# A four-stage chain on one core: the values of the first batch ahead of its scores, its silu behind the first sum, and the branch numbers chosen one batch later

## The chip, the cores and the metric

The kernel runs on one core of a Trainium2 chip. The metric is the device time of one execution in microseconds (us), as the median of several runs. The engines are named as the profile names them: PE (TensorE, matrix products; PEld is its weight load), DVE (VectorE), ACT (ScalarE), POOL (GpSimd) and SP (SyncE, which issues most of the DMAs). Each engine works through its own queue in order.

## The reference

The reference passes `x`, 16 batches of 256 tokens by 256 features in float32, through four layers. Cut to what matters:

```python
# layer 0: adapter with one of 16 experts per batch, then layer norm
hidden = gelu(x @ down_W.T + down_b)
hidden = hidden @ expert_W[idx].T + expert_b[idx] + domain_emb[idx]
x = layernorm(hidden @ up_W.T + up_b + x) * ln_gamma + ln_beta
# layer 1: conditioned transformer block, 16 heads of 16
emb = silu(sin_emb(timestep)) @ W_ada + b_ada         # sin and cos of 128 angles
scale, shift = split(emb, 2)
x = ln(x) * (1 + scale) + shift
q, k, v = x @ Wq + bq, x @ Wk + bk, x @ Wv + bv
scores = q k^T / 4 + attention_bias; masked with -inf  # the bias is 16 x 256 x 256 per batch
x = x + softmax(scores) v @ Wo + bo
h = ln(x) * g2 + beta2
x = x + gelu2(h @ W1 + b1) @ W2 + b2                   # 1024 hidden
# layer 2: one of three branches per batch (two or three products), then layer norm
x = layernorm(x + branch[condition](x)) * gamma + beta
# layer 3: finite differences along both axes, one time step
out = maximum(f + dt * df(f), 0)
```

## The kernel before

Each batch is held as two halves of 128 tokens by 256 features. The work is written as generators, each of which runs over the batches: `adapt` (layer 0, two batches at a time: matmuls into p_h, p_e and p_u, and the sum `x <- p_u, x`), `prepare` (both layer norms), `project` (transposition c_t, then queries c_q, keys c_k and values c_v), `weigh` (scores c_s for four heads at a time, the bias added and the maximum taken on DVE, the exponential on ACT), `attend` (transposition of the weights into c_pt, its copy c_pts, and the product c_c with the values c_va), `divide` (the softmax's denominator and the product with Wo), `enter` and `feed` (the feed-forward part), `end` (layer 2) and `step` (layer 3). A "quarter" of a batch is the four heads that one turn of `weigh` takes.

The order of the instructions on every engine is fixed while the program is built. `Flow.run` is a small planner: it keeps a clock for each engine with the costs that the generators state (`flow.pe(1.75)`), and picks the next generator among those whose condition holds and whose data and PSUM bank are due. Among these the smallest priority goes first. Each generator is added with a start priority and a number by which its priority grows with the PE time that it has used:

```python
    flow.add(adapt(), -3.31, 1.2)
    flow.add(enter(), -0.18, 0.44)
    flow.add(step(), 4.65, 7.0)
```

So a changed start number, or a changed cost stated to the planner, moves instructions of every generator from there on. The planner also chooses by its clocks whether DVE or ACT does certain operations: the normalization (`normalized`, L433 on DVE or L438 on ACT), the copy out of a transposition (`taken_up`, L472 or L474) and the bias of the feed-forward part (L940 or L938).

The places that the change touches:

- `timestep()` (L358 to L364) computes sine, cosine and tanh on ACT and then, on DVE, the two instructions that make the silu of the embedding (L362, L363). `adapt` calls it for the first pair, ahead of p_u, so the two DVE instructions stand ahead of the first sum (L582). The silu is what the matmuls of `condition` (L500, into ps_a) wait for.
- `choose()` turns the 16 branch numbers into row indices and selected biases, with 13 small DVE instructions (in the profile: L284 to L289 with c_f and c_row, L975 to L985). `prepare` calls it in its turn for batch 1, ahead of that batch's statistics. Its results are read by `load_branch(0)`, which `weigh` calls after the last quarter of batch 0, and by `end`.
- `weigh` begins with batch b once ("prepare", b) is done; `project` sets this after the keys, and ("values", b) after the values. So the scores of the first quarter can stand ahead of the values' product:

```python
            if m % 4 == 0:
                yield lambda: ("prepare", b) in done
```

Batch 0's scores start with matmuls that add the mask (L735, with ident_b). For later batches the mask is added to the bias tiles (`side`) in memory, by DMAs that POOL issues (L517). POOL also adds up_b to each x (`biased`, L529) once its load has landed, and takes the reciprocal square roots of the layer norms (L421 to L425, with tiles rs and nb).

The matmuls named `idle` (L222) multiply zeros while PE has nothing else to do.

Of the kernel before, what the change touches and what calls it, by code (L numbers as in the profile page):

```python
# [170 lines left out]
def chain_kernel(ctx: ExitStack, tc: tile.TileContext, t: dict, out: bass.AP):  # L171
# [3 lines left out]
    flow = Flow(BANKS)  # L175
# [15 lines left out]
    def chunked(w):  # L191
        return w.rearrange("(k p) n -> p k n", p=P)
# [3 lines left out]
    def misc(name, shape):  # L196
        numbers[name] = n = flow.take()
        return pp.tile(shape, F32, name=name, tag=f"m{n}")

    def free(name, at):  # L200

        flow.free_at[numbers.pop(name)] = at
        return at
# [29 lines left out]
    def columns(name):  # L233
        return cols[:, COLUMN[name][0] : COLUMN[name][1]]
# [6 lines left out]
    def load_turned(p):  # L241

        arrives["t", p] = flow.clock["PE"] + 9.0 if p else 0.0
        xts[p] = xp.tile([P, 2, NC, S], F32, name=f"xt{p}", tag="xt", bufs=1)
        for i in range(2):
            nc.sync.dma_start(out=xts[p][:, i], in_=chunked(t["x_t"][2 * p + i]))
# [111 lines left out]
    def timestep():  # L358
        for i, red in enumerate((sine, cosine)):
            nc.scalar.activation(emb[:, i, :], red, AF.Sin)  # L360
        nc.scalar.activation(th, emb, AF.Tanh, scale=0.5)
        nc.vector.tensor_scalar(emb, emb, 0.5, None, ALU.mult)  # L362
        nc.vector.scalar_tensor_tensor(silu, th, 1.0, emb, ALU.add, ALU.mult)  # L363
        flow.dve(0.25, flow.act(3.4))  # L364


    rows_a = load("rows_a", rows(t["rows_a"]), [P, 5 * D])
# [12 lines left out]
    def spread_mask(b):  # L380
        negs[b] = wp.tile([P, NC, S], BF16, name=f"neg{b}", tag="neg", bufs=2)
        nc.gpsimd.tensor_scalar(negs[b], m8s.pop(b), MASKED, None, ALU.mult)
        flow.pool(1.6)
# [96 lines left out]
    done = set()  # L480
    ready, ys, stats2, lns, hts, stats3 = {}, {}, {}, {}, {}, {}

    def expert_bias():

        ps_b = misc("ps_b", [2 * A, B // 2])
        for i in range(2):
            half = ps_b[i * A : (i + 1) * A, :]
            nc.tensor.matmul(half, e_rows[:, :A], e_hot[: E + 2, i::2], start=True, stop=False)
            nc.tensor.matmul(half, e_rows[:, A:], e_hot[: E + 2, i::2], start=False, stop=True)
        nc.vector.tensor_copy(e_add, ps_b)  # L490
        return free("ps_b", flow.dve(0.2, flow.pe(0.5)))
# [35 lines left out]
    def biased(b):  # L527
        x = xs[b]
        nc.gpsimd.tensor_tensor(x, x, up_b.unsqueeze(1).to_broadcast([P, NC, D]), ALU.add)  # L529
        flow.pool(1.35, arrives["x", b])  # L530
        done.add(("x", b))

    def adapt():

        for p in range(B // 2):
            yield lambda: p in e_ws and (p == 0 or ("normal", 1) in done)
            yield arrives.get(("t", p), 0.0)
            parts = [slice(i * A, (i + 1) * A) for i in range(2)]
            w, xt = e_ws.pop(p), xts.pop(p)
            ps_h = misc(f"p_h{p}", [2 * A, S])  # L540
            for k in range(NC):
                for i in range(2):
                    nc.tensor.matmul(
                        ps_h[parts[i]], w_down[:, k, :], xt[:, i, k, :], start=k == 0, stop=k == NC - 1
                    )
            h1 = xp.tile([2 * A, S], F32, name=f"a_h1{p}", tag="a_h1", bufs=1)
            nc.scalar.activation(h1, ps_h, AF.Gelu, bias=columns("down_b"))
            at = free(f"p_h{p}", flow.act(0.47, flow.pe(1.0), "gelu"))
            if p == 0:
                nc.scalar.dma_start(out=w_qkv, in_=chunked(t["W_qkv"]))  # L550
                expert_bias()
            yield at
            if p == 0:
                biased(0)
                spread_mask(0)
            ps_e = misc(f"p_e{p}", [2 * A, S])
            for i in range(2):
                nc.tensor.matmul(ps_e[parts[i]], w[parts[i]], h1[parts[i]], start=True, stop=True)
            h2 = xp.tile([2 * A, S], F32, name=f"a_h2{p}", tag="a_h2", bufs=1)
            nc.vector.tensor_scalar(h2, ps_e, e_add[:, p : p + 1], None, ALU.add)  # L560
            at = free(f"p_e{p}", flow.dve(0.4, flow.pe(0.5)))
            if p and 2 * p + 2 < B:
                load_turned(p + 1)
                load_expert(p + 1)
            if p:
                yield lambda: ("x", 2 * p + 1) in done
            yield at, 2
            if p == 0:
                timestep()
                idle(256)  # L570
            ps_u = [misc(f"p_u{2 * p + i}", [P, NC, D]) for i in range(2)]
            for c in range(NC):
                for i in range(2):
                    nc.tensor.matmul(
                        ps_u[i][:, c, :], h2[parts[i], c * P : (c + 1) * P], up[parts[i]], start=True, stop=True
                    )
            at = flow.pe(1.0)
            for b in (2 * p, 2 * p + 1):
                if b == 1:
                    yield lambda: ("normal", 0) in done  # L580
                x = xs[b]
                nc.vector.tensor_tensor(x, ps_u[b % 2], x, ALU.add)  # L582
                adapted[b] = free(f"p_u{b}", flow.dve(0.7, at))
                done.add(("adapt", b))
                yield 0.0, 0

    def prepare():
        for b in range(B):
            yield lambda: ("adapt", b) in done
            x, at = xs.pop(b), adapted.pop(b)  # L590
            yield at, 0
            flow.spent += 0.75
            if b + 2 < B:
                load_x(b + 2)
                if b == 0:
                    load_turned(1)
                    load_expert(1)
            if b == 1:
                choose()
            stat, at = take_stats(f"0_{b}", x, at)  # L600
            if b == 0:
                condition()
                idle(512, 512, 512, 512)
            yield at, 0
            tmp = xp.tile([P, NC, D], F32, name=f"b_tmp{b}", tag="b_tmp", bufs=1)
            at = normalized_affine(x, x, stat, ln0_g, ln0_b, tmp, b == 0)
            yield at, 0
            stat, at = take_stats(f"1_{b}", x, at)
            if b == 0:
                conditioned()  # L610
                masked.update((m, 0.0) for m in range(4))
            yield at, 0
            if b > 1:
                yield lambda: ("turned", b - 2) in done
            ln = xp.tile([P, NC, D], F32, name=f"c_ln{b}", tag="c_ln", bufs=2)
            lns[b] = ln, normalized(ln, x, stat, b == 0)
            flow.spent += 1.5
            for n in (1, 2) if b == 0 else (b + 2,) if b + 2 < B else ():
                biased(n)
            done.add(("normal", b))  # L620
# [98 lines left out]
    def weigh():  # L719

        at = 0.0
        for m, (b, half, par) in enumerate(QUADS):
            if m % 4 == 0:
                yield lambda: ("prepare", b) in done
            _, qz, k_t, _, sums = ready[b]
            ps = []
            for i in range(4):
# [159 lines left out]
    def enter():  # L887
        for b in range(B):
            yield lambda: ("finish", b) in done
            stat, at = stats2.pop(b)  # L890
            yield at, 0
            y = ys[b]
            ln = hp.tile([P, NC, D], F32, name=f"d_ln{b}", tag="d_ln", bufs=1)
            yield normalized(ln, y, stat)
            if b > 1:
                yield lambda: ("widen", b - 2) in done
            ps_t = misc(f"d_t{b}", [P, NC, S])
            at = transposed(ps_t, ln)
            h_t = hp.tile([P, NC, S], F32, name=f"d_ht{b}", tag="d_ht", bufs=2)
            for k in range(NC):  # L900
                nc.scalar.activation(
                    h_t[:, k, :], ps_t[:, k, :], AF.Identity, bias=ln2_b[:, k : k + 1], scale=ln2_g[:, k : k + 1]
                )
            for c in range(NC):
                nc.gpsimd.tensor_tensor(y[:, c, :], y[:, c, :], b2, ALU.add)
                flow.pool(0.7)
            hts[b] = h_t, free(f"d_t{b}", flow.act(0.9, at))
            done.add(("enter", b))
# [263 lines left out]
            free(f"e_d{b}", at)  # L1172
            done.add(("step", b))

    flow.add(adapt(), -3.31, 1.2)
    flow.add(prepare(), -2.34, 2.25)
    flow.add(project(), -0.45, 5.7)
    flow.add(weigh(), 0, 21.2)
    flow.add(attend(), 0.9, 11.3)
    flow.add(enter(), -0.18, 0.44)  # L1180
    flow.add(feed(), 2.55, 13.9)
    flow.add(end(), 3.08, 3.95)
    flow.add(step(), 4.65, 7.0)
    flow.run()

def _arrays(inputs):
# [79 lines left out]
```

## Time and profile before

| | |
|---|---|
| time, median of 3 runs | 912.29 us (911.93 to 915.16) |
| the profiled execution: its time | 912.22 us |
| the profiled execution: its span, first to last instruction | 910.4 us |
| mean granted PE clock | 0.990 |
| PE busy | 869.3 us (95%) |
| DVE busy | 636.2 us (70%) |
| ACT busy | 544.1 us (60%) |
| POOL busy | 377.4 us (41%) |
| moved by DMA | 163.25 MB, mean 179 GB/s |

A line of the timeline gives the start and the length in us, the engine, the line of the kernel, the operation, the tile written and the tiles read (`out<-in`) with shapes, and how many instructions were merged (x4). In brackets stands the idle time of the engine ahead of it and what ended that idle time. A line of the table by stage gives the stretch, its length, the busy time of each engine with the number of instructions, and at the end the granted PE clock, the mean busy share of the DMA engines and GB/s. Buffer numbers are left out of tile names.

### The profile page before, as it was taken

What the parts mean: (1) busy time and instruction counts of PE and PEld (TensorE: products, weight loads), DVE (VectorE), ACT (ScalarE), POOL (GpSimd) and SP (SyncE); (2) the same over time, 40 slices, a digit from 0 to 9 for tenths busy, and PEclk for the clock granted to TensorE, in tenths of its full rate; (3) what the DMA queues carried; (4) which work ended last, traced back from release to release, by engine and by line L of the source; (5) the groups of instructions that cost most, each with busy time, mean ns of one, the idle gap of its engine ahead of it and who ended that gap; (6) DMA issues with size and microseconds to landing.
All of it is one profiled execution on the core that took longest, in us unless ns stands there. A gap on an engine that the chain in (4) does not pass through costs nothing. (4 is left out here: it accounts for less than half of the span.)

```text
span 910.4 us, 18249 instructions
## 1 busy us (share of the span) xinstructions
PE 869.3 (95%) x6184; PEld 668.7 (73%) x6184; DVE 636.2 (70%) x2087; ACT 544.1 (60%) x1537; POOL 377.4 (41%) x514
## 2 busy tenths in 40 slices
PE   7889998999999999999999999999999999999996
PEld 3557676777878777676877777787778778776875
DVE  5677867778777867757758686866768676767443
ACT  2576857576664767557765665847557474756230
POOL 3353455445416353351627245542446332422231
PEclk9999999999999999999999999999999999999998
DMA  8599977777888668778478777765857776670000
GB/s 274 166 267 316 285 166 191 183 200 191 203 204 201 179 166 221 217 185 209 125 191 222 179 193 175 190 166 161 195 152 181 180 203 173 176 190 31 13 30 23
DMA packets 130973, 163.25 MB, mean 179 GB/s; under 512 B 12714, under 2 KB 94780, under 8 KB 130876
## 3 DMA queue, kind: packets, MB, share of 16 engines
q0 software_dynamic: 31680, 62.92, 34.0%
q1 hardware_dynamic: 97920, 96.92, 33.5%
q10 hardware_dynamic: 1275, 2.19, 0.7%
q8 instruction: 52, 0.85, 0.4%
q14 instruction: 46, 0.37, 0.1%
HBM read 94.89 MB, written 4.19 MB: 109 GB/s over the span
## 5 line engine op out<-in xcount | busy, mean ns | idle before, releaser
L769 ACT ACTIVATE c_pr<-c_sc,c_mx 128x256 f32<-128x256 f32 x512 | 255.2, 500 | 207.5 <-DVE c_mx L758 203.9
L758 DVE CUSTOM_DVE_ANT_0 c_sc<-c_s,side 128x256 f32<-128x256 f32 x512 | 193.8, 417 | 35.7 <-PE c_s L740 20.2
L472 DVE COPY c_pts<-c_pt 128x512 f32<-128x512 f32 x206 | 137.0, 683 | 21.8 <-PE c_pt L464 21.2
L464 PE MATMUL c_pt<-ident,c_pr 128*128 128x128 f32 x1024 | 144.7, 278 | 7.4 <-ACT c_pr L769 3.6
L464 PEld LDWEIGHTS c_pt<-ident,c_pr 128*128 128x128 f32 x1024 | 114.3, 141 | 43.3 <-issue 14.5
L421 POOL TENSOR_SCALAR rs<-mv 128x2 f32<-128x2 f32 x64 | 14.2, 222 | 279.7 <-DVE mv L418 278.9
L924 PE MATMUL d_f<-d_ht,w 128*128 128x256 f32 x512 | 122.9, 383 | 4.0 <-DVE c_mx L758 2.2
L954 PE MATMUL d_o<-w,d_z 128*128 128x256 f32 x512 | 116.3, 381 | 0.1
L517 POOL DMA_DIRECT2D side<-neg x60 | 82.2, 1379 | 76.6 <-DMA side<-in_side 48.9
L924 PEld LDWEIGHTS d_f<-d_ht,w 128*128 128x128 f32 x512 | 92.7, 190 | 18.7 <-DVE c_mx L758 3.7
L954 PEld LDWEIGHTS d_o<-w,d_z 128*128 128x128 f32 x512 | 94.9, 190 | 14.5 <-issue 1.9
L769 ACT ACTIVATION_READ_ACCUMULATOR c_pr<-c_sc,c_mx 128x1 f32 x512 | 96.2, 188 | 0.0
L740 PE MATMUL c_s<-c_kt,c_qz 32*128 32x256 f32 x1024 | 77.6, 401 | 4.8 <-DVE x L582 1.9
L823 PE MATMUL c_c<-c_pts,c_va 128*32 128x256 f32 x1024 | 74.1, 386 | 2.7 <-DVE c_pts L472 2.5
L740 PEld LDWEIGHTS c_s<-c_kt,c_qz 32*128 32x128 f32 x1024 | 48.9, 184 | 24.5 <-issue 9.7
L962 DVE SCALAR_TENSOR_TENSOR y<-d_o,y 128x256 f32<-128x256 f32 x32 | 13.6, 425 | 63.3 <-PE d_o L954 63.3
L823 PEld LDWEIGHTS c_c<-c_pts,c_va 128*32 128x32 f32 x1024 | 27.9, 109 | 36.9 <-issue 17.9
L943 ACT ACTIVATE d_f<-d_z 128x512 f32<-128x512 f32 x64 | 38.3, 598 | 27.0 <-DVE d_z L940 26.3
L940 DVE TENSOR_SCALAR d_z<-d_f,cols 128x256 f32<-128x256 f32 x94 | 41.0, 477 | 16.2 <-PE d_f L924 16.0
L422 POOL TENSOR_TENSOR rs<-rs,inv_sqrt 128x2 f32<-128x2 f32 x64 | 45.9, 717 | 5.3
L947 DVE SCALAR_TENSOR_TENSOR d_z<-d_f,d_z 128x512 f32<-128x512 f32 x64 | 43.4, 677 | 1.8 <-ACT d_f L943 1.8
L1029 POOL TENSOR_TENSOR y<-y,d_bout 128x256 f32<-128x256 f32 x32 | 23.6, 790 | 47.1 <-PE d_t L464 32.1
(156 smaller groups left out, 1539.7 us busy)
## 6 DMA issues: line engine op xcount, KB each, us to landing
side<-in_side SPq DMA_DIRECT2D x256, 256.0 KB, 5.3
side<-neg POOLq DMA_DIRECT2D x60, 1024.0 KB, 8.1
d_w<-in_W_branch SPq DMA_DIRECT2D x16, 512.0 KB, 4.4
xt<-in_x_t SPq DMA_DIRECT2D x16, 256.0 KB, 6.1
x<-in_x SPq DMA_DIRECT2D x16, 256.0 KB, 5.9
out<-e_o SPq DMA_DIRECT2D x15, 256.0 KB, 3.7
w<-in_W SPq DMA_DIRECT2D x2, 1024.0 KB, 7.5
d_bout<-in_bl_branch SPq DMA_DIRECT2D x16, 128.0 KB, 4.5
```

The source lines that it names most:

```text
L422: nc.gpsimd.tensor_tensor(rs, rs, inv_sqrt, ALU.pow)
L464: nc.tensor.transpose(ps[:, k, c * P : (c + 1) * P], src[:, c, k * P : (k + 1) * P], ident)
L472: nc.vector.tensor_copy(dst, ps)
L517: nc.gpsimd.dma_start(out=sides[m].rearrange("p (h c) k -> p h (c k)", h=HB), in_=negs[m // 4].rearrange("p c k -> p (c k)").unsqueeze(1). ...
L740: nc.tensor.matmul(ps[i][:, c, :], qz[rows32, par, half, c * P : (c + 1) * P], k_t[rows32, half, :], start=b > 0, stop=b > 0 or c == NC - 1,)
L758: nc.vector.tensor_tensor_reduce(out=sc[:, c, :], in0=ps[i][:, c, :], in1=sb[:, i * NC + c, :], scale=-1.0, scalar=3.0e38, op0=ALU.add, op ...
L769: nc.scalar.activation(pr[:, c, :], sc[:, c, :], AF.Exp, bias=mx[:, c : c + 1], scale=-1.0, accum_out=sums[:, c, h : h + 1],)
L823: nc.tensor.matmul(ps_c[32 * i : 32 * i + 32, :], va[:, k, 4 * half + i, 2 * par : 2 * par + 2, :].rearrange("p e d -> p (e d)"), turned[i ...
L924: nc.tensor.matmul(ps_f[:, i, :], w1[:, k, f * P : (f + 1) * P], h_t[:, k, :], start=k == 0, stop=k == NC - 1,)
L940: nc.vector.tensor_scalar(z[:, i, :], ps_f[:, i, :], b1[:, f : f + 1], None, ALU.add)
L947: nc.vector.scalar_tensor_tensor(z, ps_f, 1.0, z, ALU.add, ALU.mult)
L954: nc.tensor.matmul(ps_o, us[f // 2][:, f % 2, c * P : (c + 1) * P], w2[:, f, :], start=f == 0, stop=f == NF - 1,)
```

## The change

The two DVE instructions of the silu are taken out of `timestep()` into a function `silus()`, which `adapt` calls behind the sum of batch 0. `choose()` is called in `prepare`'s turn for batch 2 instead of batch 1. `weigh` begins with batch 0 once its values are done; for the other batches its condition is the same. Three start numbers of the planner are changed. The costs stated to the planner for the silu are split in the same way: ACT's 3.4 stays in `timestep()`, DVE's 0.25 moves, and no longer waits for ACT's clock. The numbers and shapes of the matmuls and of the DMAs stay the same; across DVE and ACT, the planner's choice between the two changes for some instructions.

```diff
@@ -359,9 +359,12 @@
         for i, red in enumerate((sine, cosine)):
             nc.scalar.activation(emb[:, i, :], red, AF.Sin)
         nc.scalar.activation(th, emb, AF.Tanh, scale=0.5)
+        flow.act(3.4)
+
+    def silus():
         nc.vector.tensor_scalar(emb, emb, 0.5, None, ALU.mult)
         nc.vector.scalar_tensor_tensor(silu, th, 1.0, emb, ALU.add, ALU.mult)
-        flow.dve(0.25, flow.act(3.4))
+        flow.dve(0.25)
@@ -580,6 +583,8 @@
                 x = xs[b]
                 nc.vector.tensor_tensor(x, ps_u[b % 2], x, ALU.add)
+                if b == 0:
+                    silus()
                 adapted[b] = free(f"p_u{b}", flow.dve(0.7, at))
                 done.add(("adapt", b))
                 yield 0.0, 0
@@ -595,7 +600,7 @@
                 if b == 0:
                     load_turned(1)
                     load_expert(1)
-            if b == 1:
+            if b == 2:
                 choose()
             stat, at = take_stats(f"0_{b}", x, at)
@@ -721,7 +726,7 @@
         for m, (b, half, par) in enumerate(QUADS):
             if m % 4 == 0:
-                yield lambda: ("prepare", b) in done
+                yield lambda: ("prepare" if b else "values", b) in done
             _, qz, k_t, _, sums = ready[b]
@@ -1172,15 +1177,15 @@
-    flow.add(adapt(), -3.31, 1.2)
+    flow.add(adapt(), -3.24, 1.2)
     flow.add(prepare(), -2.34, 2.25)
     flow.add(project(), -0.45, 5.7)
     flow.add(weigh(), 0, 21.2)
     flow.add(attend(), 0.9, 11.3)
-    flow.add(enter(), -0.18, 0.44)
+    flow.add(enter(), -0.02, 0.44)
     flow.add(feed(), 2.55, 13.9)
     flow.add(end(), 3.08, 3.95)
-    flow.add(step(), 4.65, 7.0)
+    flow.add(step(), 4.83, 7.0)
```

## The prediction

> **What bounds the kernel now.** I read the page's engine row, then a table of TensorE's (PE) busy time by stage, then the timeline of the stage that the change touches.
>
> ```profile
> PE 869.3 (95%) x6184; PEld 668.7 (73%) x6184; DVE 636.2 (70%) x2087; ACT 544.1 (60%) x1537; POOL 377.4 (41%) x514
> ```
>
> ```profile
> 21.00:100.00 79.00, 69.49 (x518) 0.96 0.87 258
> ...
> 850.00:910.40 60.40, 50.69 (x248) 0.94 0.07 24
> ```
>
> ```profile
> 100.00:850.00 750.00, 732.74 (x5363) 572.22 (x5362) 541.77 (x1770) 474.49 (x1356) 318.72 (x420) 1.00 0.71 181
> ```
>
> PE is the bound. After the stretch come its length, PE's busy time and, at the row's end, the granted clock and DMA. PE idles 9.5 us from 21 to 100, 17.3 us in all of 100 to 850, 9.7 us in the last 60. The change leaves the number of matmuls as it is, so it can only move these idle pieces and the slow-clock stretches. Now the opening, with what each gap waited for in brackets:
>
> ```profile
> 13.54 0.18 DVE L362 TENSOR_SCALAR smalls<-smalls 128x32 f32<-128x32 f32 x1 [1.95 <-ACT smalls L361]
> ...
> 13.86 0.68 DVE L582 TENSOR_TENSOR x<-p_u,x 128x512 f32<-128x512 f32 x1
> ...
> 26.35 1.27 POOL L529 TENSOR_TENSOR x<-x,rows_a 128x512 f32<-128x512 f32 x1 [3.80 <-DMA x<-in_x]
> ...
> 28.75 0.73 DVE L433 TENSOR_SCALAR b_tmp<-x,mv,rs 128x256 f32<-128x256 f32 x2 [1.21 <-POOL rs L422]
> ...
> 32.12 0.76 DVE L700 TENSOR_TENSOR c_va<-c_v,rows_a 128x256 f32<-128x256 f32 x2 [1.17 <-PE c_v L691]
> ```
>
> ```profile
> 29.01 1.15 PE L740 MATMUL c_s<-c_kt,c_qz 32*128 32x256 f32 x16 [1.71 <-ACT c_kt L679]
> 30.09 1.99 PE L691 MATMUL c_v<-w_qkv,c_xt 128*128 128x256 f32 x8
> 31.92 0.60 PE L464 MATMUL c_pt<-ident,c_pr 128*128 128x128 f32 x4
> 34.96 0.33 PE L464 MATMUL c_pt<-ident,c_pr 128*128 128x128 f32 x1 [2.44 <-ACT c_pr L769]
> ...
> 63.60 0.33 PE L464 MATMUL c_t<-ident,c_ln 128*128 128x128 f32 x1 [1.20 <-ACT c_ln L438]
> ...
> 66.50 1.57 PE L823 MATMUL c_c<-c_pts,c_va 128*32 128x256 f32 x10 [1.29 <-DVE c_pts L472]
> 67.99 3.12 PE L648 MATMUL c_q<-c_xt,w_qkv 128*128 128x256 f32 x8
> ```
>
> Three waits of the first batch are named: scores for keys (1.71), the second transposition for its softmax (2.44), and on VectorE (DVE) the first sum behind the silu, which stands for 1.95 behind ScalarE's (ACT's) tanh.
>
> **The change, part by part.** (x(n) is batch n's activations, weigh(m,i) head i of quarter batch m.)
>
> *Silu behind the first sum.* The sum's inputs are there at 12.61 (POOL's add, 11.35 + 1.26) and 12.78 (PE's p_u, 11.64 + 1.14), so it runs from about 12.8 instead of 13.86. The silu pair (0.32) then stands at 13.54 as before, since tanh ends at 13.50; the statistics start near 13.95 instead of 14.58: 0.63 won on DVE and POOL. On PE it is worth less. The warm-up matmuls (L222, idle) hold PE from 15.92 to 21.17, and the first transposition c_t began at 21.16; only its wait for the second half goes. I take 0.2 for PE (bounds 0 and 0.63).
>
> *Branch numbers out of batch 1.* `choose()` held DVE from 23.19 to 25.49: 2.30 us ahead of x(1)'s statistics, themselves ahead of c_qz. Without it c_qz starts when c_q is there, about 24.5 instead of 26.57, and the keys' copy c_kt near 26.4 instead of 28.49. But x(1) gains nothing from it: POOL's rs for x(1) is queued behind POOL's add for x(2), and that waits for x(2)'s DMA until 26.35, which no part of the change moves. So b_tmp stays at 28.75 and x(1) is normalized at 32.19 as now.
>
> *Values ahead of the scores.* c_v (2.0 on PE) goes to where PE waited for keys: c_k ends near 26.2, c_v 28.0, the mask matmuls 29.0, the scores run 29.0 to 30.0: their start stays within 0.1 us of the 29.01 of before. So the 1.71 is filled, but c_v no longer covers the softmax after it: PE idles from 30.0 until c_pr is exponentiated at 31.7. DVE then does c_va (29.45), weigh(0,0) at 30.2 (30.18 before), x(1)'s second statistics at 32.25, bound by POOL's 32.19, and weigh(0,1) at 33.35 (33.87 before). The order now has weigh(0,2) directly behind, at 34.05 instead of 35.13, and c_ln of x(1) comes at 35.4 instead of 36.64. On ACT two table loads and a gelu (1.28 + 0.47 + 1.28) stay ahead of the fourth exponential. PE's p_h of the next pair is moved into the softmax wait (from 35.92 to about 32.3).
>
> *The clock.* These rows show PE's busy time right after the stretch's length, and the granted clock as the third number from the end.
>
> ```profile
> 28.00:32.00 4.00, 2.99 (x25) 2.38 (x26) 1.51 (x6) 2.42 (x8) 3.48 (x5) 1.00 0.04 9
> 32.00:36.00 4.00, 1.40 (x11) 0.80 (x11) 3.71 (x15) 1.50 (x5) 1.90 (x6) 1.00 0.00 0
> 36.00:40.00 4.00, 4.00 (x21) 2.82 (x22) 2.71 (x8) 3.94 (x8) 0.87 (x1) 0.57 0.15 50
> ```
>
> In 36 to 40 the clock is 0.57, and there p_h takes 1.78 (1.08 at 54.43) and c_t 1.06 (0.66 at 89.79). [...] The longest gap here is 2.44[...]. After the change PE is busy about 2.0 us of 32 to 36 (rest of a transposition, p_h, another one), against 1.40 before and 2.61 in 64 to 68, which was followed by 0.71 in 68 to 72. I therefore let c_t and the mask of the next quarter run slow again. Worked through to c_k of batch 1 (45.84 before), the lead is 1.2 us by the row; with full clock[...], 2.1. I take 1.2 and keep 2.1 for the range.
>
> *Branch numbers into batch 2.* The same 2.30 us of DVE, no DMA of its own, now stand between weigh(1,3) and x(2)'s statistics, about 47.4 to 49.7. Queued behind are those statistics, the copy c_pts of a transposition and weigh(2,0), near 51.5 instead of 52.26. PE had no idle worth a bracket from 43 to 63, and DVE is busy 12.33 of 15 there, so I charge 0.3 (bounds 0 and 1.2). SP issues the load of x(4) behind four side loads and w2 instead of ahead of them: near 51.5 and not 45.04. It lands in about 6.0, and POOL adds to x(4) only at 61.46; I cost that nothing. Without that cover of some 4 us POOL, and the mask addition queued behind it there, would be late by what is missing.
>
> *The order after that.* The planner's costs and the three start numbers (adapt, enter, step) move nearly every row from there on. In the order after the change the second batch's gather c_c stands ahead of c_t of x(2), not behind it, and c_ln of x(2) is done on DVE, not on ACT behind eight exponentials. So c_c and more transpositions cover the 1.36 us wait for c_ln (1.20 and 0.16). What is at stake from 57 to 76 is that, the 1.29 for c_pts and 1.13 of slow clock in c_q (3.12 against 1.99): 3.8 us. I take 2.6, bounds 0 and 3.8. From 100 to 850 DVE gets 18 more instructions (8 normalizations of 0.365, 5 copies of 0.683, one of 0.69, 4 bias adds of 0.477: 8.9 us) and ACT as many fewer. PE's listed waits there name DVE for 10.1 us and ACT for 4.1, in pieces of at most 1.9, so no row tells a sign: I take 0, bounds -6 and +8. The last 157 matmuls, from batch 14's output product on, stand in the same order in both: 0.
>
> **Sum.** -1.2 + 0.3 - 2.6 = -3.5 us. The profiled execution took 912.22 (span 910.4 and 1.8 around it), 0.07 under the median of 912.29; so 908.7.
>
> **The rivals.** *The middle falls well too.* The new order loses less than the 17.3 us of 100 to 850: with 5 us fewer 903.7. For it: the pieces are accidents of order, and ACT, relieved of 18 instructions, answers sooner. Against: DVE pays for that.
>
> *The lead is handed back.* The masked sides, or w1 and w2, arrive when they did: DMA's share is 1.02 in 57 to 76 and 1.09 in 76 to 100. Then little but 0.7 us remains: 911.5. Against it: no PE gap from 21 to 100 names a DMA.
>
> *DVE late, slower.* `choose()` in front of x(2)'s statistics delays the weighing that all PE work of the second batch needs, by its whole 2.30 less the lead of 1.2, the gains at 57 to 76 do not come, and the 8.9 us of DVE work moved from ACT raise PE's waits on DVE (10.1) by half: 1.1 + 5 = 6.1, 918.3. It decides once PE's waits on DVE in 100 to 850 pass about 14 us. For it: DVE is the releaser in most of them, and 203.9 us of ACT's waiting are for DVE's c_mx. Against: DVE is idle 28% of that stretch.
>
> *Nothing of what it says.* Weigh(0,0) stays at 30.2 and x(1) stays bound by x(2)'s DMA; if the clock dips longer as well, the opening gives nothing. This lies in the second rival's figure.
>
> **How the numbers follow.** 0.5% (4.6 us), about what a measurement of this kernel can tell from no change, puts the bounds at 907.7 and 916.9. The likeliest, 0.46, is 908.7 with its own range 904.5 to 912.5: 0.20 faster, 0.25 same, 0.01 slower. Middle falls well 0.20, all faster. Lead handed back 0.09: 0.08 same, 0.01 slower. DVE late 0.25: 0.23 slower, 0.02 same. Together 0.40, 0.35 and 0.25. The range, 900 to 920, takes in the full clock and the bounds of the middle down to -5 and up to about +8.
>
> **What would show it.** Right: c_v between c_k and the mask matmuls with no gap; scores near 29.0; weigh(0,1) near 33.4; POOL's x(2) still waiting for DMA near 26.35; the third quarter's scores 1 to 2 us under 51.0; PE idle from 21 to 100 near 7 instead of 9.5. Wrong: PE idle in 100 to 850 away from 17.3 by over 5, which would outweigh the opening; or PE waiting for c_mx or c_pts between 47 and 60.

## The result, and the profile after

The changed kernel takes 918.44 us (median of 5 runs, 916.23 to 921.17); the kernel before, beside it, 912.27 (5 runs, 910.42 to 915.16). The ratio is 1.0059 with a 95% interval of 1.0035 to 1.0083: slower, by 6.2 us at the medians. The forecast was 908.7.

The profiled execution of after was the longest of its five, 921.17 (span 919.4). From the page, the engine row first:

```profile
PE 872.3 (95%) x6184; PEld 668.7 (73%) x6184; DVE 648.3 (71%) x2105; ACT 535.5 (58%) x1519; POOL 377.0 (41%) x514
```

The span is 9.0 us longer than before's 910.4. PE's busy time accounts for 3.0 of it (872.3 against 869.3). The matmuls are the same 6184, and this part is slow clock: the stretches at half clock cost PE 11.2 us in this trace and 8.2 in before's. PE's idle time accounts for the other 6.0 (919.4 - 872.3 = 47.1, against 41.1), which is about the difference of the medians. The 18 instructions that left ACT for DVE are there (2105 and 1519). The table by stage, for PE alone (length, busy time, then granted clock, DMA share and GB/s), of before and then of after:

```profile
21.00:42.00 21.00, 16.04 (x105) 0.92 0.47 144
42.00:57.00 15.00, 14.71 (x118) 1.00 0.88 291
57.00:76.00 19.00, 16.26 (x118) 0.91 1.02 265
76.00:100.00 24.00, 22.50 (x184) 1.00 1.09 330
170.00:850.00 680.00, 665.69 (x4887) 1.00 0.70 179
```

```profile
21.00:42.00 21.00, 16.41 (x106) 0.92 0.49 150
42.00:57.00 15.00, 13.62 (x106) 1.00 0.92 294
57.00:76.00 19.00, 16.40 (x141) 1.00 0.88 235
76.00:100.00 24.00, 21.82 (x168) 1.00 1.09 326
170.00:850.00 680.00, 661.91 (x4855) 1.00 0.70 180
```

Length less busy time is PE's idle time. From 21 to 42 it falls by 0.4 us; then it rises by 1.1, falls by 0.1 and rises by 0.7. So the opening, which was to gain, has 1.2 us more idle PE by 100 than before. From 170 to 850 it rises from 14.3 to 18.1. The rest (to 21, from 100 to 170, behind 850) adds 0.8, 0.0 and 0.2; the 0.8 need not come of the change, since e11 below, with before's instructions up to 32, idles 6.5 to 21, against before's 4.6.

The opening in after's timeline, first DVE, then POOL, then PE:

```profile
12.77 0.69 DVE L585 TENSOR_TENSOR x<-p_u,x 128x512 f32<-128x512 f32 x1 [1.56 <-POOL x L532]
...
26.90 1.27 POOL L532 TENSOR_TENSOR x<-x,rows_a 128x512 f32<-128x512 f32 x1 [5.24 <-DMA x<-in_x]
...
29.29 0.73 DVE L436 TENSOR_SCALAR b_tmp<-x,mv,rs 128x256 f32<-128x256 f32 x2 [4.13 <-POOL rs L425]
```

```profile
25.69 1.89 PE L696 MATMUL c_v<-w_qkv,c_xt 128*128 128x256 f32 x8
27.42 1.04 PE L740 MATMUL c_s<-neg,ident_b 128*128 128x256 bf16 x8
28.38 1.15 PE L745 MATMUL c_s<-c_kt,c_qz 32*128 32x256 f32 x16
31.72 0.33 PE L467 MATMUL c_pt<-ident,c_pr 128*128 128x128 f32 x1 [2.19 <-ACT c_pr L774]
...
50.11 1.15 PE L745 MATMUL c_s<-c_kt,c_qz 32*128 32x256 f32 x16
52.28 0.63 PE L467 MATMUL c_pt<-ident,c_pr 128*128 128x128 f32 x4 [1.02 <-DVE c_pts L475]
```

The values stand without a gap ahead of the mask matmuls, and the scores start 0.6 us sooner than before. PE then waits 2.19 for the softmax. At 50.11 the third quarter's scores are 0.9 us ahead of before's 51.0. Behind them is a wait that before did not have: 1.02 for DVE. The cause is on DVE:

```profile
48.09 0.17 DVE L284 CAST c_f<-tok 128x16 f32<-128x16 int32 x1
...
49.97 0.51 DVE L990 SCALAR_TENSOR_TENSOR b_sel<-is_c,cols,b_sel 128x16 f32<-128x16 f32 x2
50.39 0.42 DVE L420 BATCH_NORM_STATS2 st<-x 128x6 f32<-128x256 f32 x1
...
51.47 0.66 DVE L475 COPY c_pts<-c_pt 128x512 f32<-128x512 f32 x1
```

`choose()` holds DVE for 2.30 us, and the copy that PE waits for is queued behind it and the statistics.

### The profile page after: what moved, and what is told of

Read it like the earlier page. It is cut to its first block, busy times and chain, and to the rows that moved or that the text cites. A ratio compares the mean times of both kernels' runs of the same rounds, so it can differ in the third digit from the quotient of the medians.

```text
span 919.4 us, 18249 instructions
## 1 busy us (share of the span) xinstructions
PE 872.3 (95%) x6184; PEld 668.7 (73%) x6184; DVE 648.3 (71%) x2105; ACT 535.5 (58%) x1519; POOL 377.0 (41%) x514
## 3 DMA queue, kind: packets, MB, share of 16 engines
q10 hardware_dynamic: 1275, 2.19, 0.7%
## 5 line engine op out<-in xcount | busy, mean ns | idle before, releaser
L467 PE MATMUL c_pt<-ident,c_pr 128*128 128x128 f32 x1024 | 147.1, 278 | 13.2 <-ACT c_pr L774 5.6
L475 DVE COPY c_pts<-c_pt 128x512 f32<-128x512 f32 x211 | 140.4, 683 | 14.6 <-PE c_pt L467 14.3
```

The lines of the kernel that those rows point to most:

```text
L467: nc.tensor.transpose(ps[:, k, c * P : (c + 1) * P], src[:, c, k * P : (k + 1) * P], ident)
L475: nc.vector.tensor_copy(dst, ps)
```

## The experiments

Kernels of one group share a chip and their runs of before. "In before's order" means that the costs told to the planner stay as in before, so every instruction that is not moved by hand keeps its place on every engine.

**e1_starts**: before, with only the three start numbers of the change.

```diff
-    flow.add(adapt(), -3.31, 1.2)
-    flow.add(enter(), -0.18, 0.44)
-    flow.add(step(), 4.65, 7.0)
+    flow.add(adapt(), -3.24, 1.2)
+    flow.add(enter(), -0.02, 0.44)
+    flow.add(step(), 4.83, 7.0)
```

> The kernel before with only the three new start numbers (adapt, enter, step); the first batch's instructions stand as before. Theory A (the order of everything behind the first batch costs the time, and the start numbers choose it): slower by 4 to 8 us, about 916 to 920, with PE's idle time from 100 to 850 above 20 us against 17.3. Theory B (the moves inside the first batches cost it: choose() on DVE ahead of x(2)'s statistics, or the softmax left uncovered): as before, 912 +- 2, since none of these moves is in it.

**e2_edits**: after with the start numbers of before (the planner orders the rest). Against after:

```diff
-    flow.add(adapt(), -3.24, 1.2)
+    flow.add(adapt(), -3.31, 1.2)
...
-    flow.add(enter(), -0.02, 0.44)
+    flow.add(enter(), -0.18, 0.44)
...
-    flow.add(step(), 4.83, 7.0)
+    flow.add(step(), 4.65, 7.0)
```

> The changed kernel with the old start numbers: the three moves of the first batches, and the order behind them as the planner makes it from there. Theory A: about as before or up to 3 us faster, 909 to 913, if the old start numbers give a good order behind a moved opening too; if each reordering costs by chance, anything up to 918. Theory B: slower like the whole change, 916 to 920.

**e3_dve_moves**: silu behind the first sum, and choose() in batch 2, in before's order.

```diff
+        flow.dve(0.25, flow.act(3.4))
+
+    def silus():
         nc.vector.tensor_scalar(emb, emb, 0.5, None, ALU.mult)
         nc.vector.scalar_tensor_tensor(silu, th, 1.0, emb, ALU.add, ALU.mult)
-        flow.dve(0.25, flow.act(3.4))
...
+                if b == 0:
+                    silus()
...
-            if b == 1:
+            if b == 2:
                 choose()
```

> The kernel before with only the silu behind the first sum and choose() moved to batch 2, the planner being told of them as before, so that every other instruction keeps its place on its engine. Theory A: 911 to 912.5, nothing or a little won, since x(1) still waits for POOL's add of x(2). Theory B: slower by 2 to 5 us, because choose() delays the weighing of the second quarters.

**e4_frozen**: e3 and the values of batch 0 issued just ahead of its first mask matmuls, in before's order otherwise. `valued` is the product c_v and its two bias additions, taken out of `project` as they were.

```diff
+            if m == 0:
+                early["bank"] = n = flow.free_at.index(min(flow.free_at))
+                valued(0, ready[0][0], vas[0], pp.tile([P, NC, D], F32, name="c_v0", tag=f"m{n}"))
             if b == 0:
                 for i in range(4):
```

> All three moves of the first batches (silu, choose, values ahead of the scores), with the planner told of them as before, so that from the second quarter on every engine keeps the order of before. Theory A: 910 to 912, the lead of 1 to 2 us that the prediction gave to the opening. Theory B: slower by 4 to 8 us, 916 to 920, as the whole change.

Measured, as ratio to before: e1 1.0107 (1.0074 to 1.0139, 923.59 us), e2 1.0045 (1.0034 to 1.0057), e3 1.0047 (1.0029 to 1.0065), e4 1.0037 (1.0021 to 1.0052). So neither theory holds alone. The start numbers cost time with no edit at all. The edits cost some 4 us with the start numbers of before, and also with every other instruction left in place. The parts do not add up: e1 alone lost more than the whole change. PE's table by stage, for 170 to 850, of e1 and of e2:

```profile
170.00:850.00 680.00, 661.39 (x4822) 1.00 0.69 179
```

```profile
170.00:850.00 680.00, 665.53 (x4884) 1.00 0.71 180
```

With the new start numbers PE idles 18.6 us there, with the old ones 14.5, as before (14.3). After, with 18.1, is among the first. So the start numbers bring this loss, and the edits do not. e1's profiled run (927.93, its longest) also had a mean clock of 0.981, and PE was busy 11.5 us longer than in before's. Of this the clock makes at most 8.8, as an estimate from the two traces: 0.019 of its span of 926.2 is 17.6 us, against 8.8 lost in before's 910.4 at 0.990. But at a clock of 0.995 another of its runs still took 918.53, 8 us over before's runs at 0.994, and the 4.3 us of idle PE are half of that: some 4 us of e1's loss stay unexplained.

**e5_choose_only**: before, with choose() in batch 2 and nothing else.

```diff
-            if b == 1:
+            if b == 2:
                 choose()
```

> The kernel before with choose() alone moved to batch 2; every other instruction keeps its order. Theory C (choose's 2.3 us on DVE now stand ahead of weighing that the mask matmuls of the third quarter wait for: a PE gap of some 1.5 us near 51 us, as in the two runs with all DVE moves): slower by 1 to 4 us, 914 to 917. Theory D (the loss comes from the emptier PE of 29 to 36 us and the clock that falls behind it, whatever the order on DVE): 912 to 914, since nothing was moved out of that stretch.

**e6_silu_values**: silu and values moved as in e4, choose() left in batch 1. Against e4:

```diff
-            if b == 2:
+            if b == 1:
                 choose()
```

> Silu and values moved as in the change, choose() left in batch 1, the order behind them kept. Theory C: 911 to 913.5, the loss is gone with choose. Theory D: 916 to 918, with a mean granted clock of about 0.984 as in the run with all three moves, because PE still runs empty behind the first scores.

**e7_frozen_fed**: e4 with four matmuls of zeros, 512 columns each, in the two waits for the softmax; nothing reads their product.

```diff
+            if m == 0:
+                feed_clock(2)
...
+                if n == 0:
+                    feed_clock(2)
                 at = free(f"c_pt{n}", taken_up(p_t, ps_p, at))
```

> All three moves with the order behind them kept, and four matmuls of zeros of 512 columns put into the two softmax gaps of PE (two behind the first scores, two behind the first transposition); they add work that nobody waits for. Theory D: the fall of the clock near 34 us goes or gets shorter, mean clock up from 0.984 to 0.988 or more, time down by 2 to 4 us to 913 to 915. Theory C: clock and time stay within 1 us of 917.3, or it is slower by the 1.7 to 3.4 us of the added matmuls if they are in the way.

**e8_silu_values_fed**: e6 with the same four matmuls (the same diff).

> Silu and values moved, choose() in batch 1, and the four matmuls of zeros. If C and D each explain a part, this is the fastest of the four: 908 to 912, under the kernel before. If neither holds: 916 to 918.

Measured: e5 1.0043 (1.0031 to 1.0054), e6 1.0000 (0.9984 to 1.0017), e7 1.0009 (0.9996 to 1.0021), e8 0.9992 (0.9979 to 1.0006). Silu and values gave nothing and cost nothing. choose() alone cost 4 us. Its gap, in the timeline of e5 (e3, e4 and e7 have it too, 1.47 or 1.48; in e6 and e8, with choose() in batch 1, it is absent):

```profile
51.70 0.98 PE L735 MATMUL c_s<-neg,ident_b 128*128 128x256 bf16 x6 [1.48 <-DVE c_mx L758]
```

PE's table from 42 to 57, of e5 and then of e6, has the same:

```profile
42.00:57.00 15.00, 13.33 (x100) 1.00 0.82 254
```

```profile
42.00:57.00 15.00, 14.70 (x122) 1.00 0.91 291
```

The gap is 1.5 us, and e5 lost 4 (917.23 us). The rest goes with the clock: the median granted clock was 0.984 in e3, e4 and e5, against 0.988 in before and e6, and 0.004 of 917 us is 3.7 us of PE work at most. At a like clock less is lost: nine of e5's runs, at 0.984, took 917.1 on average, and the only two of before's at 0.984 on that chip 915.7. So theory C gives the gap. Theory D, as it was put, failed twice: e5 lost time although nothing was moved out of 29 to 36, and e6 lost none although PE was emptier there than in before (busy for 3.5 of the 7 us against 4.4; e4 2.5) and the clock fell as low as in e4. These are the rows of e4 and then of e6:

```profile
32.00:36.00 4.00, 1.50 (x6) 0.67 0.00 0
36.00:40.00 4.00, 4.00 (x18) 0.50 0.01 3
```

```profile
32.00:36.00 4.00, 1.84 (x9) 0.69 0.00 0
36.00:40.00 4.00, 4.00 (x19) 0.50 0.19 59
```

With zeros in the softmax waits the clock there held, as e7's rows show, and the median clock rose (0.990 in e7, 0.9895 in e8):

```profile
32.00:36.00 4.00, 3.76 (x18) 1.00 0.00 0
36.00:40.00 4.00, 4.00 (x44) 1.00 0.27 73
```

The distance between choose() late and early shrank to 0.0017 (e7 less e8), 1.6 us: about the gap itself, though the two intervals overlap. So the clock carries much of the rest of a late choose()'s loss; which slow stretches it brings was not settled.

The last group asks whether that also explains after itself, and e2.

**e9_after_choose_early**: after with choose() back in batch 1, all else in after's order.

```diff
-            if b == 2:
+            if b == 1:
                 choose()
```

> After with choose() back in the turn of batch 1, every other instruction in after's order. Theory C (choose() ahead of the third quarter's weighing costs the change its time, in any order): the bracket for a DVE release between 50 and 59 goes, PE is busy over 1 us more from 42 to 57, and the time falls by 2.5 to 4 us against after, to 1.0015 to 1.003 of before. Theory O (the new order costs the time by itself): it stays at 1.005 to 1.007, whatever becomes of that gap.

**e10_after_fed**: after with the four matmuls of zeros (the diff of e7).

> After with two products of zeros of 512 columns on PE behind the first scores and two behind the first transposition of the weights (four matmuls, nothing reads them), nothing else moved. Theory D (emptier PE from 29 to 36, with the clock behind it): granted clock 1.00 in 21 to 42, mean clock up by 0.003 to 0.005, time down by 2 to 4 us against after, to about 1.002 to 1.004 of before. If the clock only falls elsewhere instead: no more than 1 us.

**e11_before_fed**: before with three such matmuls behind the first transposition of the weights.

```diff
+                if n == 0:
+                    feed_clock(3)
```

> Before with three products of zeros of 512 columns behind the first transposition of the weights, where PE waited 2.44 us; nothing else moved. Theory D: the slow stretch near 36 to 40 goes, and with it 1 to 2 us: 0.998 to 0.999. If the slow stretch comes of the opening's sum and not of this gap: it moves to another place and the time stays at 1.000.

**e12_edits_choose_early**: e2 with choose() back in batch 1 (the diff of e9).

> After with the start numbers of before and choose() back in the turn of batch 1: silu and values moved, the planner free to order what follows. Theory C: 1.000 to 1.0015, since the moved silu and values alone gave 1.000 and choose() is back. Theory O: the planner's order from 57 to 120 costs by itself (PE idle over 11 us of 20 to 120, with waits over 1 us near 77, 93 and 108): 1.003 to 1.005.

Measured: e9 1.0042 (1.0027 to 1.0057), e10 1.0042 (1.0027 to 1.0057), e11 0.9989 (0.9974 to 1.0004), e12 1.0038 (1.0023 to 1.0053). e9 lies between both expectations: taking choose() back is worth 1.5 us (1.0042 against 1.0059, intervals that overlap), and the wait at 52 is gone. What is left is the order: from 170 to 850 e9 idles as after does.

```profile
170.00:850.00 680.00, 661.41 (x4848) 1.00 0.69 179
```

e10's zeros bring 1.00 in 21 to 42 and a median clock of 0.992, for about 1.5 us, less than expected. In e12 choose() is early, and yet 3.5 us of e2's 4.1 remain: theory O. From 20 to 120 PE idles 12.1 us in e12 and 12.7 in e2, against 9.6 in before. The largest waits of e12 on PE, then one on DVE:

```profile
74.19 1.25 PE L828 MATMUL c_c<-c_pts,c_va 128*32 128x256 f32 x10 [2.61 <-DVE c_pts L475]
91.80 0.98 PE L561 MATMUL p_e<-a_h,e_w 64*64 64x256 f32 x4 [1.24 <-ACT a_h L550]
108.52 3.30 PE L653 MATMUL c_q<-c_xt,w_qkv 128*128 128x256 f32 x8 [1.63 <-DVE c_mx L763]
```

```profile
72.75 0.42 DVE L763 CUSTOM_DVE_ANT_0 c_sc<-c_s,side 128x256 f32<-128x256 f32 x1 [2.87 <-DMA side<-in_side]
```

The gather c_c waits for a copy c_pts; the copy is queued on DVE behind a weighing, and that waits 2.87 for its bias tile to arrive. e2 has the same pair (2.22 on PE at 77.03 behind 2.49 on DVE at 75.60). But this pair takes the place of before's waits for c_ln and c_pts (1.36 and 1.29), so it adds next to nothing. The wait of 1.63 ahead of c_q at 108.52 is new: e2 has it too (1.63 at 108.53), before does not. That it makes e12's loss is a reading of the two traces; no run takes it away.

e11 lost the slow stretch of 36 to 40 (its clock there was 1.00) and ran 1.8 us ahead (its wait for c_ln ended at 61.79, before's at 63.60), and still ended within 0.0011 of before, in an interval that holds 1. In its profiled run (915.14, over 3 us above its median, so not the usual case) the lead went as follows, POOL first, then DVE, then PE:

```profile
87.85 1.36 POOL L526 DMA_DIRECT2D side<-neg  x1 [2.63 <-DMA side<-in_side]
...
93.43 0.42 DVE L767 CUSTOM_DVE_ANT_0 c_sc<-c_s,side 128x256 f32<-128x256 f32 x1 [4.05 <-DMA side<-neg]
...
94.36 1.09 PE L473 MATMUL c_pt<-ident,c_pr 128*128 128x128 f32 x4 [3.83 <-DVE c_mx L767]
```

POOL issues the DMA that adds the mask once the bias tile has come from memory (2.63 us of waiting), DVE waits for that DMA (4.05), and PE waits for DVE (3.83). Neither e8 nor e11 can be told from before, so no version here beats it.

## Why the prediction was wrong

*Silu behind the first sum: right.* Sum at 12.77 (12.8 forecast), statistics at 13.70 (13.95). The first transposition c_t started at 20.85 instead of 21.16, within the bounds; but p_u, ahead of the change, already stood 0.37 sooner in this execution (11.27 instead of 11.64), so no gain on PE is shown. With the values it made 1.0000 in e6.

*Values ahead of the scores: right.* c_v ended 0.4 us sooner than forecast, the scores started at 28.38 (29.0), and the wait for the softmax came where it was put. x(1) stayed bound by the load of x(2): POOL waited 5.24 for it until 26.90, b_tmp was at 29.29 and the second weighing at 33.87, exactly where it had been before (33.35 forecast; the load came 0.55 later in this execution).

*The clock and the lead: nearly right.* 36 to 40 ran at 0.65, behind waits of at most 2.19 us, as the row of before had said (0.57, behind at most 2.44). The third quarter's scores were 0.9 us ahead, with 1.2 forecast. That the clock fell at this place was in part luck: e12, whose longest wait there was 1.93, stayed at 1.00 (last section).

*Branch numbers into batch 2: this step failed.* It was priced at 0.3 (bounds 0 and 1.2) because PE had no idle worth a bracket there. The right delay was even named (weighing and a copy behind 2.30 us on DVE), but PE's lack of idle time was read as cover when it only meant that PE was being supplied just in time. The wait came to 1.02 in after, within the bounds, and to 1.48 in before's order. As a whole the late choose() cost about 1.5 us in after (e9) and 4 in before's order (e5), where the clock went with it: outside the bounds. PE's wait for c_pts between 47 and 60, which the prediction had named as a sign of its being wrong, was this one. The other part of this step, the load of x(4) costed at nothing, held: from 40 to 130 no wait of over 0.5 us for it shows on DVE, ACT or POOL.

*The order from 57 to 76: this step failed too.* Forecast 2.6. The slow clock did leave this stage (the row went from 0.91 to 1.00, and c_q at 69.56 took 2.02 instead of 3.12), but that is no gain of the order: with before's order there, e5, e6 and e7 show 1.00 too, and e4 and e8 0.82. And after ran at half clock elsewhere, from 157 to 164 and from 327 to 331 (0.59 in 156 to 160, 0.65 in 328 to 332), where before did not. PE's idle time only fell from 2.74 to 2.60. The waits for c_ln and c_pts that went were replaced by three others:

```profile
57.42 1.05 PE L828 MATMUL c_c<-c_pts,c_va 128*32 128x256 f32 x10 [0.77 <-ACT c_pts L477]
...
64.60 0.64 PE L828 MATMUL c_c<-c_pts,c_va 128*32 128x256 f32 x6 [1.15 <-DVE c_cts L860]
65.88 1.05 PE L828 MATMUL c_c<-c_pts,c_va 128*32 128x256 f32 x10 [0.65 <-DVE c_pts L475]
```

*The second rival was dismissed on the wrong evidence.* "No PE gap from 21 to 100 names a DMA" is true of after as well, and yet one of its gaps goes back to DMAs, two engines away:

```profile
90.81 1.36 POOL L520 DMA_DIRECT2D side<-neg  x1 [3.96 <-DMA side<-in_side]
...
96.71 0.42 DVE L763 CUSTOM_DVE_ANT_0 c_sc<-c_s,side 128x256 f32<-128x256 f32 x1 [2.32 <-DMA side<-neg]
...
98.79 1.05 PE L828 MATMUL c_c<-c_pts,c_va 128*32 128x256 f32 x10 [0.94 <-DVE c_pts L475]
```

POOL's row was in the trace of before, with 1.67 us for the same wait at 90.34. It grew to 3.96: POOL was done with its earlier work 1.8 us sooner (86.85 instead of 88.68), and the tile came 0.5 later. So 0.94 of the 2.2 us that PE idles from 76 to 100 is this rival's. Another 1.03, ahead of p_u at 85.91, is not: there PE waits for a weighing on DVE, which stood behind a product of PE's own. That the loads themselves are the limit rests on these waits and on the DMA share of 1.09 in 76 to 100 of both kernels; a kernel with fewer bytes there was not tried.

*The middle, taken at 0: the largest miss.* It lay within the stated bounds, -6 and +8. This term was put at nothing because no row told a sign, although the start numbers move every row of it. PE's idle time from 170 to 850 grew by 3.8 in after and by 4.0 to 4.3 in e1, e9 and e10, all with the new start numbers; in e2 to e8, e11 and e12, with the old ones, it was within 0.3 of before. PE's listed waits there, in after:

```profile
PE d_f L929 <- DVE c_pts L475: 2.4, 3, 0.8
PE c_pt L467 <- ACT d_f L948: 1.7, 1, 1.7
PE c_pt L467 <- DVE c_mx L763: 1.3, 1, 1.3
PE e_z L1121 <- DVE e_b L1110: 1.2, 2, 1.0
PE c_o L871 <- DVE c_mx L763: 1.0, 2, 0.5
```

(In all, times and longest, in us.) Summed by engine, DVE's went from 7.5 to 9.4 and ACT's from 4.1 to 5.3. No single wait carries it. Since ACT's part grew too although ACT lost 18 instructions, the moved work alone is not the explanation. In e1 only 8 instructions moved, and PE idled as much (DVE's waits 11.6, ACT's 3.6). So the start numbers are shown to be the cause, and why this order waits more stays open; which of the three numbers does it was not tried.

The third rival, "DVE late, slower", gave 918.3 for 1.1 of choose() and 5 of the middle, and the kernel took 918.44. Its two terms are near what was measured, 1.1 from 42 to 57 and 3.8 from 170 to 850. But its reason was not: PE's waits on DVE from 100 to 850 went from 10.1 to 10.8, far from the 14 at which it was to decide. So that its sum fell on the measured time is in part luck.

## What to carry to other kernels

Where the bounding engine never waits, ask how late its suppliers deliver: an instruction put into a supplier's queue is free only up to the slack between delivery and need, and "no gap" may mean no slack. A lead in the opening is worth what the next late supplier leaves of it, so follow the waits of the engines behind the bound (here POOL for a bias tile, DVE for POOL's DMA) before it is entered in a sum. With an order that a planner makes, compare an edit with all else frozen in place, and price the reordering apart from it. Where the clock is at stake, the length of the longest gap is no safe guide: behind one and the same wait of 1.91 us the clock was full in before and half in e4 (next section).

## What the runs showed of the hardware

The clock fell after waits of about 2 us, and not each time. With 1.81 and 2.46 us of PE work in 28 to 32 and 32 to 36, and no gap over 2.19, after ran at 0.65 in 36 to 40; with 1.91 and 2.45, and no gap over 1.93, e12 stayed at full clock:

```profile
28.00:32.00 4.00, 1.91 (x21) 1.00 0.01 3
32.00:36.00 4.00, 2.45 (x16) 1.00 0.00 0
36.00:40.00 4.00, 3.88 (x35) 1.00 0.38 108
```

Even one and the same wait did both. Here are the ten matmuls behind it, in before at full clock (1.00 in 150 to 160) and in e4 at half (0.67 over 160 to 170):

```profile
156.73 1.13 PE L740 MATMUL c_s<-c_kt,c_qz 32*128 32x256 f32 x10 [1.91 <-DVE x L582]
```

```profile
160.24 2.07 PE L755 MATMUL c_s<-c_kt,c_qz 32*128 32x256 f32 x10 [1.91 <-DVE x L584]
```

In before's clock record the slow stretches between 20 and 880 us run from 36.17 to 39.58 and from 66.89 to 70.30, in after's from 37.24 to 40.65, from 156.70 to 163.53 and from 327.37 to 330.78, all at half clock. In the 4 us ahead of them PE was busy for 1.40, 1.83, 2.42, 2.81 and 2.33 us. But 2.29 us of work in 25.34 to 29.34 of before, and 1.89 in 29.83 to 33.83 of after, were followed by full clock. So in these two traces PE stood idle for over 1.1 of the 4 us ahead of every slow stretch, but neither its busy time nor its longest gap tells behind which of such places the clock falls. What decides it was not shown.

Between executions of one kernel the mean clock differs: of before's runs beside e1 to e4, the two at a mean clock of 0.994 took 910.3 us and the one at 0.984 took 915.7. For this kernel that is a scatter as large as the effects looked for, so gains of a few us have to be read from PE's idle time as well as from the total.
